# Two graph blocks on one core: the opening, the order of the steps and the last groups rearranged

## The chip, the cores and the metric

The kernel runs on one core of one Trainium2 chip. The metric is the device time of one execution in microseconds (us). Engines are named as in the profile: PE is TensorE (PEld its weight loads), DVE is VectorE, ACT is ScalarE, POOL is GpSimd, SP is SyncE, which here only issues DMAs.

## The reference, cut to what matters

There are 128 graphs of 128 nodes with 256 features, and an adjacency of zeros and ones. Two layers follow each other.

```python
# layer 0: attention with 8 heads; only edge types 0 and 1 occur in adj
q, k = src @ Wq + bq, src @ Wk + bk
attn = softmax(q k^T / sqrt(32))
out  = sum_r (attn * (adj == r)) @ (src @ Wv[r] + bv[r])
x = LN(src + out @ Wo + bo)
x = LN(x + gelu(x @ W1 + b1) @ W2 + b2)            # 256 -> 1024 -> 256
# layer 1: two graph attention steps, then a relu feed-forward
def gat(h, W, a):                                   # softmax over axis 1, the source nodes
    Wh = h @ W
    e = leaky_relu(Wh @ a[:256] + (Wh @ a[256:])^T, 0.2)
    return softmax(where(adj > 0, e, NEG), axis=1) @ Wh
h = LN(x + gat(gat(x, W1g, a1), W2g, a2))
out = LN(h + relu(h @ w_ff1 + b_ff1) @ w_ff2 + b_ff2)
```

## The kernel before

**Tiling.** All is in float32. Four graphs (512 tokens) make a group; there are 32 groups. One group's work is cut into generators, and each `yield` ends a step:

- `projections` has 8 steps: two for the queries, two for the keys (L560), four for the values (`pv`, L570, with the bias added on DVE at L574).
- `attention` has 12: for each pair of graphs `scores` (matmuls L588, four exponentials L594), `masked` (DVE, L602), and three of `sums` (denominators L615, weighted values L624, reciprocals and products on DVE); then two with the output projection L662, the residual and its statistics.
- `ffn` has 22: 14 with the products of the first matrix (`product`, L400, each four passes of 256 columns) and 8 of the second (`product2`, L409, 16 passes of 128). It is a seven-product form of a 2x2 block product, so most products add into one PSUM bank, `seeded`, and ACT copies stand between them (L438, L445 `p7`, L449 `p16`, L472). `first_ffn` uses gelu, `second_ffn` relu.
- `layer1` has 12: two with `Wh` (L713), `spread`, three of `edges`, the product L726, `spread`, three of `edges`, the product L738 with residual and statistics.
- `norm` has 4: `root` (DVE L324, POOL power L325), `normed` (L333 on DVE, then L338 on ACT, one instruction for each graph; for the last norm L343 on DVE), and two of `scaled` (DVE, L356). `turned` transposes the normalised group on PE (L290), copies it on ACT (L293) and forms sums for the next products (L378 to L381, DVE).

**Graph weights.** `graph_weights` makes one matrix `wu` from the weights of both graph steps, so that one product gives what both need. It runs once, in the opening, with columns on DVE (L92), four transposes (L254) and a product (L262) on PE. Its sources lie in `temp`, which is the later `hT` buffer.

**Spread.** `spread` lays one number per node along the free axis in all partitions: a transpose on PE (L672), a copy on DVE (L674), a DMA to HBM (L677) and a DMA back to all partitions (L678). The 64 return trips are issued on SP.

**Order.** `manual_schedule` keeps the order of the text on every engine. `in_order` takes a list of generators, with a count of steps where it is over one, and runs them; so the kernel's schedule is written out by hand. In the loop over `g`, the first list holds `first_ffn` of group g+1 (`f1`) with the graph steps of group g (`l1`); the second holds `second_ffn` of group g (`f2`) with the attention of group g+2 (`at`, `pr`). PSUM tiles with tag `s` come from a ring of four banks; each new tile waits until the one four before it has been read.

Of the kernel before, what the change touches and what calls it, by code (L numbers as in the profile page):

```python
# [23 lines left out]
P = 128  # L24
# [5 lines left out]
class Weights:  # L30
# [55 lines left out]
    def columns(self, wt, arow, scr, name):  # L86

        nch, d = wt.shape[1], wt.shape[2]
        wa = self.tile([P, nch, 2], "wa_" + name)
        for c in range(nch):  # L90
            for s in range(2):
                self.nc.vector.scalar_tensor_tensor(  # L92
                    scr, wt[:, c, :], 1.0, arow[:, s * d : (s + 1) * d],
                    op0=ALU.mult, op1=ALU.mult, accum_out=wa[:, c, s : s + 1],
                )
        return wa
# [10 lines left out]
def fast_pass(ctx, tc, a, out):  # L107
# [47 lines left out]
    def entered(g):  # L155

        xt = load_xT(g)
        ad, xr = load_rest(g)
        return dict(xt=xt, ad=ad, x=xr, g=g)
# [3 lines left out]
    first = dict(g=0, xt=load_xT(0))  # L163
# [49 lines left out]
    gw1, gw2 = (k.w("L1_gnn_W" + s, cut(NCH, D)) for s in "12")  # L213
    a1, a2 = (k.row("L1_gnn_a" + s, t=cut(2 * D)) for s in "12")
# [7 lines left out]
    w2 = forms("L0_gnn_W2")  # L222
    g2c, be2c = k.col("L0_gnn_g2"), k.col("L0_gnn_beta2")
# [13 lines left out]
    NU = D + 4  # L237
    wu = k.tile([P, NCH, NU], "wu")

    def graph_weights():  # L240

        scr = cut(D)
        wa1 = k.columns(gw1, a1, scr, "1")
        wa2 = k.columns(gw2, a2, scr, "2")
        rhs = cut(NCH, D + 2)
        nc.vector.tensor_copy(rhs[:, :, :D], gw2)
        nc.vector.tensor_copy(rhs[:, :, D : D + 1], wa2[:, :, 1:2])
        nc.vector.tensor_copy(rhs[:, :, D + 1 : D + 2], wa2[:, :, 0:1])
        gw1T = cut(NCH, D)
        yield  # L250
        for m in range(NCH):
            pt = mm_tile(f"pgt_{m}")
            for c in range(NCH):
                nc.tensor.transpose(  # L254
                    pt[:, c * P : (c + 1) * P], gw1[:, c, m * P : (m + 1) * P], k.ident
                )
            nc.scalar.copy(gw1T[:, m, :], pt[:, :D])
        yield
        for m in range(NCH):
            pu = mm_tile(f"pgw_{m}")  # L260
            for c in range(NCH):
                nc.tensor.matmul(  # L262
                    pu[:, : D + 2], gw1T[:, c, m * P : (m + 1) * P], rhs[:, c, :],
                    start=(c == 0), stop=(c == NCH - 1),
                )
            nc.scalar.copy(wu[:, m, : D + 2], pu[:, : D + 2])
            nc.vector.tensor_copy(wu[:, m, D + 2 : D + 3], wa1[:, m, 1:2])
            nc.vector.tensor_copy(wu[:, m, D + 3 :], wa1[:, m, 0:1])
        yield
# [57 lines left out]
    def normed(S, i, bs=slice(0, G)):  # L327


        x, mv, rs = S["x"], S["mv", i], S["rs", i]  # L330
        if i < 3:
            sh = small.tile([P, G], F32, tag="sh", name=f"sh_{i}_{S['g']}")
            nc.vector.scalar_tensor_tensor(  # L333
                sh, mv[:, :, 0], -1.0, rs, op0=ALU.mult, op1=ALU.mult
            )
        for b in range(bs.start, bs.stop):
            if i < 3:
                nc.scalar.activation(  # L338
                    x[:, b, :], x[:, b, :], AF.Identity, bias=sh[:, b : b + 1],
                    scale=rs[:, b : b + 1],  # L340
                )
            else:
                nc.vector.tensor_scalar(  # L343
                    x[:, b, :], x[:, b, :], mv[:, b, 0:1], rs[:, b : b + 1],
                    op0=ALU.subtract, op1=ALU.mult,
                )
# [322 lines left out]
    def spread(columns, n):  # L669

        pr = ps_s.tile([P, T], F32, tag="s", name="pr_" + n)
        nc.tensor.transpose(pr[:G, :P], columns, k.ident)  # L672
        line = small2.tile([G, P], F32, tag="line", name="line_" + n)
        nc.vector.tensor_copy(line, pr[:G, :P])  # L674
        t = w2p.tile([P, G, P], F32, tag="spread", name="spread_" + n)
        hbm = dram.tile([G, P], F32, tag="hbm", name="hbm_" + n)
        nc.sync.dma_start(hbm, line)  # L677
        nc.sync.dma_start(t, hbm.partition_broadcast(P))  # L678
        return t
# [25 lines left out]
    def layer1(S):  # L705
# [14 lines left out]
        target = spread(wh[:, :, D + 3], n + "_0")  # L720
# [10 lines left out]
        target = spread(yh[:, :, D + 1], n + "_1")  # L731
# [42 lines left out]
    with tc.manual_schedule(engines={ET.PE, ET.Activation, ET.DVE, ET.SP, ET.Pool}):  # L774

        nc.tensor.matmul(seeded, k.ident, first["xt"][:, 0, :], start=True, stop=True)
# [3 lines left out]
        gw, pr, at = graph_weights(), projections(first), attention(first)  # L780
# [4 lines left out]
            lambda: combined(w1), (pr, 4), gw, (pr, 4), (at, 2), gw, at, lambda: combined(w2), at, gw, (at, 2), (pr1, 2), at,  # L785
            at, (pr1, 2), (at, 2), at, pr1, at, pr1, (n0, 2), lambda: turned(first, 0), (n0, 2),
# [4 lines left out]
            lambda: combined(u1), (f1, 4), at1, (f1, 4), at1, pr1, (f1, 3), (at1, 3), pr1, f1, at1, f1, at1,  # L791
            f1, f1, (at1, 3), f1, f1, at1, lambda: combined(u2), f1, at1, f1, n0_, f1, n0_, (f1, 2), lambda: turned(S1, 0), n1_, (n0_, 2),
        )
        for g in range(NG - 1):
# [8 lines left out]
            ready = (lambda: prepared(S2)) if more else (lambda: None)  # L803
            if g == 0:
                in_order((f1, 2), n1_, pr, (f1, 2), lambda: turned(S, 1), (n1_, 2))
                l1 = layer1(S)
                in_order(
                    f1, l1, f1, l1, f1, l1, (f1, 2), pr, (f1, 4), pr, f1, (l1, 3), f1, pr, f1, l1, f1,
                    l1, pr, f1, pr, f1, (l1, 3), f1, pr, f1, l1, n2, (at, 2), f1, n2, f1, n1, pr,
                    lambda: turned(S, 2), (at, 3),  # L810
                )
            else:
                n3 = norm(st[g - 1], 3)
                in_order(
                    pr, lambda: turned(S1, 0), pr, f1, f2_, n3, f1, n0_, (f1, 4), n0_, (f1, 2), n3, l1, f1, f1, l1, n3,
                    (f1, 3), pr, n3, lambda: store(st[g - 1]), f1, f1, exp, l1, l1, pr, f1, l1, f1,
                    f1, l1, n2, f1, at, n2, at, f1, pr, lambda: turned(S, 2), pr, (at, 3), f1, f1, pr, n1,
                )
            if not more:
# [3 lines left out]
                f2, pr, f2, n1, (n2, 2), f2, at, (f2, 2), lambda: turned(S1, 1), (f2, 2), at, (n1, 2),  # L823
                (f2, 2), l1, at, ready, (f2, 4), l1, f2, at, f2, l1, (f2, 2), at, at, f2, at, n0, l1, f2,
                n0, l1, gelu, f2, l1, f2,
            )
            n0_, f2_ = n0, f2
        in_order((f2, 2), n1, (f2, 2), lambda: turned(S1, 1), (n2, 2))
        l1 = layer1(S1)
        in_order(  # L830
            f2, (l1, 2), f2, l1, (n1, 2), (f2, 8), (l1, 3), f2, l1, f2, l1, (f2, 4), (l1, 3), f2, l1,
        )
        n2, n3 = norm(S1, 2), norm(S, 3)
        in_order(n2, f2, n2, (f2, 2), lambda: turned(S1, 2))
        f2 = second_ffn(S1)
        in_order((f2, 14), (n2, 2), (n3, 4), lambda: store(S), (f2, 2))
        checks()
        in_order((f2, 4))
        for p in (1, 0):
            root(S1, 3, pair(p))  # L840
            normed(S1, 3, pair(p))
# [3 lines left out]
            if p == 1:  # L845
                in_order((f2, 2))
# [18 lines left out]
def general_pass(ctx, tc, a, out):  # L865
# [46 lines left out]
    def gat_weights(s):  # L912
# [5 lines left out]
        nc.vector.tensor_copy(wt[:, :, D : D + 1], wa[:, :, 1:2])  # L918
        for c in range(NCH):
            nc.vector.tensor_copy(wb[:, c, :], wa[:, c, 0:1].to_broadcast([P, P]))  # L920
# [271 lines left out]
```

## Time and profile before

| what | value |
|---|---|
| median of 3 runs | 2836.33 us (2835.97 to 2838.88) |
| the profiled execution, its own time | 2840.0 us |
| its span, first to last instruction | 2837.9 us |
| PE busy | 2776.8 us, 98% |
| DVE, ACT, POOL busy | 77%, 55%, 6% |
| mean granted clock of TensorE | 0.991 |
| moved by DMA | 87.27 MB |

The span is the time between the first and the last instruction that the profile shows; 2.1 us of the execution's own time lie around it. The profiled execution took 3.7 us more than the median. Busy time of PE counts a matmul as long as the profile's model holds it in the array, so a busy PE isn't always one at its peak. The clock is given as a share of the full one; a 0.5 means that each pass takes twice as long.

### The profile page before, as it was taken

What the parts mean: (1) busy time and instruction counts of PE and PEld (TensorE: products, weight loads), DVE (VectorE), ACT (ScalarE), POOL (GpSimd) and SP (SyncE); (2) the same over time, 40 slices, a digit from 0 to 9 for tenths busy, and PEclk for the clock granted to TensorE, in tenths of its full rate; (3) what the DMA queues carried; (4) which work ended last, traced back from release to release, by engine and by line L of the source; (5) the groups of instructions that cost most, each with busy time, mean ns of one, the idle gap of its engine ahead of it and who ended that gap; (6) DMA issues with size and microseconds to landing.
All of it is one profiled execution on the core that took longest, in us unless ns stands there. A gap on an engine that the chain in (4) does not pass through costs nothing.

```text
span 2837.9 us, 51798 instructions
## 1 busy us (share of the span) xinstructions
PE 2776.8 (98%) x20816; PEld 2233.8 (79%) x20816; DVE 2176.8 (77%) x5068; ACT 1568.5 (55%) x3395; POOL 162.2 (6%) x153
## 2 busy tenths in 40 slices
PE   8999999999999999999999999999999999999986
PEld 4778788887888887888887887887887887888875
DVE  6677887877787877777877777778778778878765
ACT  3545555556555556555556565556556555555552
POOL 3000000000000000000000000000000000000000
PEclk9999999999999999999999999999999999999998
DMA  6010110010111010111010111000110001110000
GB/s 173 5 27 15 32 35 34 24 34 12 34 35 34 23 35 12 35 34 34 23 35 12 35 34 34 24 26 21 34 35 27 31 15 32 35 34 23 16 16 20
DMA packets 70645, 87.27 MB, mean 31 GB/s; under 512 B 8192, under 2 KB 48512, under 8 KB 70400
## 3 DMA queue, kind: packets, MB, share of 16 engines
q1 hardware_dynamic: 69568, 83.52, 9.5%
q8 instruction: 164, 2.69, 0.4%
q14 instruction: 81, 0.66, 0.1%
q10 hardware_dynamic: 832, 0.40, 0.0%
HBM read 66.99 MB, written 16.91 MB: 30 GB/s over the span
## 4 chain that ended last, share of the span: by engine, by line
PE 86%; ACT 7%; DVE 2%; issue 0%; POOL 0%; POOLq 0%; DVEq 0%; ACTq 0%
PE ph L400 14%; PE po L409 14%; PE seeded L409 12%; PE seeded L400 11%; PE pq L560 7%; PE pv L570 6%; PE pw L713 4%; PE pav L624 4%; ACT x L338 4%; PE pwo L662 4%; PE pt L290 3%; PE pden L615 2%; PE py L726 2%; PE pg L738 2%; ACT e L594 1%; PE ps L588 1%
## 5 line engine op out<-in xcount | busy, mean ns | idle before, releaser
L338 ACT ACTIVATE x<-x,sh,rs 128x256 f32<-128x256 f32 x384 | 199.4, 597 | 180.5 <-DVE sh L333 180.5
L325 POOL TENSOR_TENSOR rs<-rs,mhalf 128x4 f32<-128x4 f32 x129 | 138.8, 1076 | 2635.0 <-DVE rs L324 2225.5
L594 ACT ACTIVATE e<-ps 128x512 f32<-128x512 f32 x256 | 131.8, 601 | 209.1 <-PE ps L588 209.1
L570 PE MATMUL pv<-wv,xT 128*128 128x512 f32 x512 | 242.3, 597 | 0.3 <-ACT e L594 0.3
L400 PE MATMUL seeded<-yS,w_L_gnn_w_ff 128*128 128x256 f32 x768 | 207.3, 392 | 5.0 <-ACT seeded L472 1.3
L400 PE MATMUL seeded<-yS,w_L_gnn_W 128*128 128x256 f32 x768 | 204.0, 388 | 2.4 <-ACT seeded L472 1.3
L455 DVE TENSOR_TENSOR hT<-seeded,p 128x512 f32<-128x512 f32 x128 | 88.5, 692 | 148.3 <-PE seeded L400 148.3
L400 PE MATMUL ph<-yT,w_L_gnn_w_ff 128*128 128x256 f32 x768 | 199.0, 388 | 0.0
L310 DVE BATCH_NORM_STATS2 st<-x 128x6 f32<-128x256 f32 x512 | 192.5, 418 | 7.7
L400 PE MATMUL ph<-yT,w_L_gnn_W 128*128 128x256 f32 x768 | 194.4, 382 | 2.4 <-ACT yT L293 2.4
L409 PE MATMUL po<-w_L_gnn_W,hT 128*128 128x128 f32 x1536 | 190.1, 277 | 0.0
L409 PE MATMUL po<-w_L_gnn_w_ff,hT 128*128 128x128 f32 x1536 | 187.0, 275 | 0.0
L409 PEld LDWEIGHTS po<-w_L_gnn_w_ff,hT 128*128 128x128 f32 x1536 | 184.0, 192 | 3.2
L409 PEld LDWEIGHTS po<-w_L_gnn_W,hT 128*128 128x128 f32 x1536 | 181.7, 192 | 5.7 <-issue 0.5
L400 PEld LDWEIGHTS seeded<-yS,w_L_gnn_W 128*128 128x128 f32 x768 | 138.4, 190 | 52.7 <-issue 15.6
L400 PEld LDWEIGHTS seeded<-yS,w_L_gnn_w_ff 128*128 128x128 f32 x768 | 137.8, 190 | 48.9 <-ACT p L449 24.6
L400 PEld LDWEIGHTS ph<-yT,w_L_gnn_W 128*128 128x128 f32 x768 | 144.2, 191 | 38.0 <-ACT yT L293 10.2
L400 PEld LDWEIGHTS ph<-yT,w_L_gnn_w_ff 128*128 128x128 f32 x768 | 139.2, 191 | 38.3 <-issue 13.9
L602 DVE TENSOR_TENSOR pm<-e,adj 128x512 f32<-128x512 f32 x256 | 161.7, 693 | 4.1 <-ACT e L594 4.1
L686 ACT ACTIVATE gs<-spread,wh 128x128 f32<-128x128 f32 x128 | 40.9, 390 | 187.1 <-DMA spread<-hbm 187.1
L424 ACT ACTIVATE hT<-hT,c_L_gnn_b 128x256 f32<-128x256 f32 x256 | 109.4, 497 | 61.4 <-DVE hT L455 60.3
L570 PEld LDWEIGHTS pv<-wv,xT 128*128 128x128 f32 x512 | 90.7, 192 | 66.1 <-issue 63.6
(155 smaller groups left out, 6116.4 us busy)
## 6 DMA issues: line engine op xcount, KB each, us to landing
xT<-in_xT_dram SPq DMA_DIRECT2D x32, 512.0 KB, 7.1
x<-in_x_dram SPq DMA_DIRECT2D x32, 512.0 KB, 8.3
spread<-hbm SPq DMA_DIRECT2D x64, 256.0 KB, 4.2
out_dram<-x SPq DMA_DIRECT2D x31, 512.0 KB, 2.9
adj<-in_adjT_dram SPq DMA_DIRECT2D x32, 256.0 KB, 6.0
w_L_gnn_W<-in_L_gnn_W_dram SPq DMA_DIRECT2D x8, 256.0 KB, 7.3
w_L_gnn_w_ff<-in_L_gnn_w_ff_dram SPq DMA_DIRECT2D x8, 256.0 KB, 5.1
hbm<-line SPq DMA_DIRECT2D x64, 2.0 KB
```

The costliest lines, as they stand in the source:

```text
L310: nc.vector.bn_stats(st[:, b % 2, :], S["x"][:, b, :])
L325: nc.gpsimd.tensor_tensor(rs[:, bs], rs[:, bs], k.mhalf[:, bs], op=ALU.pow)
L338: nc.scalar.activation(x[:, b, :], x[:, b, :], AF.Identity, bias=sh[:, b : b + 1], scale=rs[:, b : b + 1],)
L400: nc.tensor.matmul(bank[:, s * TH : (s + 1) * TH], wa[:, form, 0, f * P : (f + 1) * P], m, start=start and s == 0, stop=True, skip_group_c ...
L409: nc.tensor.matmul(bank[:, s * P : (s + 1) * P], m[:, f, s * P : (s + 1) * P], wb_[:, form, f, :], start=start and s + f == 0, stop=True, ...
L560: nc.tensor.matmul(pq, w[:, c, m * P : (m + 1) * P], xt[:, c, :], start=(c == 0), stop=(c == NCH - 1),)
L570: nc.tensor.matmul(pv, xt[:, c, b * P : (b + 1) * P], wv[:, c].rearrange("p r d -> p (r d)"), start=(c == 0), stop=(c == NCH - 1),)
L594: nc.scalar.activation(e[:, s], pss[s], AF.Exp, scale=SCALE)
L602: nc.vector.tensor_mul(pm[:, s], S["e", p][:, s], S["ad"][:, pair(p), None, :].to_broadcast([P, 2, NCH, P]),)
L624: nc.tensor.matmul(pav[s * DH : (s + 1) * DH, u, c, :], v[:, d0 : d0 + DH], m[:, s, u, c, :], start=(r == 0), stop=(r == 1),)
L662: nc.tensor.matmul(po[:, s * D : (s + 1) * D], oT[:, c, b * P : (b + 1) * P], wo[:, c, :], start=(c == 0), stop=(c == NCH - 1),)
L713: nc.tensor.matmul(pw[:, :NU], yT[:, c, b * P : (b + 1) * P], wu[:, c, :], start=(c == 0), stop=(c == NCH - 1),)
```

## The change

- **Opening.** Instead of one product that waits for the first input, four products of the identity with itself fill `seeded`. The first pair's scores come directly behind the keys, ahead of the values. The graph weights leave the opening: their four loads go behind the second group's inputs and the weights `w2`, into the buffers of `wh` and `yh`, and their steps (now four: columns 1, columns 2, transposes, products) stand in the first group's feed-forward. The two extra columns of the product are now matmuls of their own. The second group's first scores, mask and sums move ahead of the first feed-forward; a gelu table is loaded ahead of it.
- **Spread.** With `direct`, `spread` is four matmuls with the broadcast column as weights and the identity as moving operand, whose result is read from PSUM. This is used for both spreads of groups 0 and 31 and for the second one of group 30.
- **Loop.** In the first list, the second of two value steps moves ahead of `turned(S, 2)`. In the second list a value step moves behind the second step of `f2` and `normed` of `n1`.
- **Last groups.** The transposes of group 30's last norm go behind `f1`'s last steps; a step of `f2` moves from before to behind the transposes of group 31; the lists from there on are written anew; the last norm is applied on ACT where only a pair is normed.

The core of the diff:

```diff
@@ entered
-        return dict(xt=xt, ad=ad, x=xr, g=g)
+        return dict(xt=xt, ad=ad, x=xr, g=g, direct={NG - 1: 0, NG - 2: 1}.get(g, 2))
@@ loads
-    gw1, gw2 = (k.w("L1_gnn_W" + s, cut(NCH, D)) for s in "12")
-    a1, a2 = (k.row("L1_gnn_a" + s, t=cut(2 * D)) for s in "12")
     wo = k.w("L0_gnn_Wo")
...
     second = entered(1)
     w2 = forms("L0_gnn_W2")
+    gw = flat(w1p.tile([P, G, NU], F32, tag="wh", name="gw"))[...]
+    ga = flat(w1p.tile([P, G, D + 2], F32, tag="yh", name="ga"))[...]
+    for i in range(2):
+        k.w(f"L1_gnn_W{i + 1}", gw[:, i])
+        k.row(f"L1_gnn_a{i + 1}", t=ga[:, i])
@@ graph_weights, last step
+            for cols, rhs in ((slice(0, D), gw[:, 1]), (slice(D, D + 2), wa2)):
+                for c in range(NCH):
+                    nc.tensor.matmul(pu[:, cols], gw1T[:, c, m * P : (m + 1) * P], rhs[:, c, :], ...)
@@ normed
-        if i < 3:
+        scalar = i < 3 or bs.stop - bs.start < G
+        if scalar:
@@ spread
+        if direct:
+            for b in range(G):
+                nc.tensor.matmul(
+                    pr[:, b * P : (b + 1) * P], columns[:, b : b + 1].to_broadcast([P, P]), k.ident,
+                    start=True, stop=True,
+                )
+            return pr.rearrange("p (b i) -> p b i", b=G)
@@ the schedule
-        nc.tensor.matmul(seeded, k.ident, first["xt"][:, 0, :], start=True, stop=True)
+        for _ in range(4):
+            nc.tensor.matmul(seeded, k.ident, over(k.ident), start=True, stop=True)
-            lambda: combined(w1), (pr, 4), gw, (pr, 4), (at, 2), gw, at, lambda: combined(w2), at, gw, (at, 2), (pr1, 2), at,
-            at, (pr1, 2), (at, 2), at, pr1, at, pr1, (n0, 2), lambda: turned(first, 0), (n0, 2),
+            lambda: combined(w1), (pr, 4), at, (pr, 2), at, (pr, 2), at, lambda: combined(w2), (at, 3), (pr1, 2),
+            (at, 2), (pr1, 2), (at, 3), pr1, at, at1, n0, n0, pr1, at1, lambda: turned(first, 0), (at1, 2),
@@ first feed-forward
-            lambda: combined(u1), (f1, 4), at1, (f1, 4), at1, pr1, (f1, 3), (at1, 3), pr1, f1, at1, f1, at1,
-            f1, f1, (at1, 3), f1, f1, at1, lambda: combined(u2), f1, at1, f1, n0_, f1, n0_, (f1, 2), lambda: turned(S1, 0), n1_, (n0_, 2),
+            gelu, lambda: combined(u1), (f1, 4), pr1, f1, f1, at1, at1, f1, pr1, f1, n0, at1, (f1, 2), n0, f1, at1,
+            (f1, 3), gwu, at1, f1, gwu, f1, at1, gwu,
+            f1, at1, f1, gwu, at1, lambda: combined(u2), f1, n0_, f1, n0_, (f1, 3), lambda: turned(S1, 0), n1_, (n0_, 2),
@@ the loop, first list from group 1 on (its last line)
-                    f1, l1, n2, f1, at, n2, at, f1, pr, lambda: turned(S, 2), pr, (at, 3), f1, f1, pr, n1,
+                    f1, l1, n2, f1, at, n2, at, f1, pr, pr, *((ahead,) if more else ()), (at, 3), f1,
+                    f1, pr, n1, *(() if more else (ahead,)),
@@ the loop, second list (its first line)
-                f2, pr, f2, n1, (n2, 2), f2, at, (f2, 2), lambda: turned(S1, 1), (f2, 2), at, (n1, 2),
+                (f2, 2), n1, pr, (n2, 2), f2, at, (f2, 2), lambda: turned(S1, 1), (f2, 2), at, (n1, 2),
@@ the last groups
-        in_order((f2, 2), n1, (f2, 2), lambda: turned(S1, 1), (n2, 2))
+        in_order(f2, n1, (f2, 2), lambda: turned(S1, 1))
-            f2, (l1, 2), f2, l1, (n1, 2), (f2, 8), (l1, 3), f2, l1, f2, l1, (f2, 4), (l1, 3), f2, l1,
+            (f2, 2), (l1, 3), f2, l1, (f2, 2), l1, n1, (f2, 2), l1, n1, (f2, 2), l1, f2, l1, n2, f2, l1, l1, n2, (f2, 3), l1, (f2, 2), l1,
-        in_order(n2, f2, n2, (f2, 2), lambda: turned(S1, 2))
+        in_order(n2, f2, n2, (f2, 3), lambda: turned(S1, 2))
-        in_order((f2, 14), (n2, 2), (n3, 4), lambda: store(S), (f2, 2))
+        in_order(f2, n3, (f2, 3), n2, n3, (f2, 4), n2, n3, (f2, 4), n3, lambda: store(S), (f2, 2))
```

In the first loop pass (g = 0) the lists are rewritten in the same way: the graph steps start after six steps of `f1` instead of four, and its end is that of the later passes. The very last norm is split: both roots come early, and pair 0 is normed while pair 1 is scaled and stored.

## The prediction

> **What bounds the kernel now.** I read the page first, then busy time by stretch, PE's waits in each stretch, and the timeline where a wait stands. By the page PE bounds the kernel at nearly full clock:
>
> ```profile
> PE 2776.8 (98%) x20816; PEld 2233.8 (79%) x20816; DVE 2176.8 (77%) x5068; ACT 1568.5 (55%) x3395; POOL 162.2 (6%) x153
> ```
>
> The stretches (bounds, length, busy time and count of PE, PEld, DVE, ACT and POOL, then clock and DMA) show where the other 2% are: PE lacks 20.0 us in the first 180, 3.9 in 2485 us of the middle, 37.3 in the last 173.
>
> ```profile
> 0.00:180.00 180.00, 159.98 (x1137) 110.81 (x1138) 114.08 (x240) 84.75 (x168) 28.79 (x29) 0.96 0.26 72
> 180.00:2665.00 2485.00, 2481.10 (x18846) 2006.67 (x18845) 1954.83 (x4552) 1413.73 (x3074) 125.62 (x116) 1.00 0.09 29
> 2665.00:2838.00 173.00, 135.67 (x836) 116.31 (x834) 107.86 (x278) 70.01 (x156) 7.75 (x8) 0.89 0.05 16
> ```
>
> A wait costs twice, for the clock follows it. Two throttled stretches, one of each end:
>
> ```profile
> 55.00:62.00 7.00, 6.80 (x17) 4.59 (x18) 4.63 (x4) 3.62 (x6) 6.69 (x6) 0.52 0.00 0
> 2785.80:2792.80 7.00, 6.37 (x17) 4.38 (x18) 1.61 (x4) 4.11 (x7) 0.00 (x0) 0.51 0.00 0
> ```
>
> Each follows a wait of about 4 us. PE's waits of the opening, then those of the end (who, for whom: us, times, longest):
>
> ```profile
> PE pt L290 <- ACT x L338: 6.0, 12, 3.8
> PE seeded L776 <- DMA xT<-in_xT_dram: 5.2, 1, 5.2
> ...
> PE pt L290 <- ACT x L338: 6.4, 8, 4.0
> PE seeded L409 <- DVE x L496: 4.8, 1, 4.8
> PE pg L738 <- DVE gs L702: 4.4, 2, 3.1
> PE py L726 <- DVE gs L702: 4.3, 1, 4.3
> ```
>
> In the middle the page shows no wait, for each is under 0.15 us by its model. The timeline shows two per period of 85.73 us. The eight transposes take 1.30 us where those at 1033.67 take 1.04; the products at 1032.70 start 1.22 us after those before them, where four passes take 0.86:
>
> ```profile
> 1016.68 1.30 PE L290 MATMUL pt<-ident,x 128*128 128x128 f32 x8
> 1031.48 1.13 PE L400 MATMUL ph<-yT,w_L_gnn_w_ff 128*128 128x256 f32 x4
> 1032.08 0.57 ACT L449 COPY p<-seeded 128x512 f32<-128x512 f32 x1
> 1032.70 1.13 PE L400 MATMUL seeded<-yS,w_L_gnn_w_ff 128*128 128x256 f32 x4
> ```
>
> The copy L449 comes late since the four normalisations L338 hold ACT from 1030.10 to 1032.18.
>
> **What the Trainium skill says.** "TensorE: Matmul & The Clock Gate", Part 1 (the HAM clock gate): the clock starts at half and rises after some 3.4 us of sustained work in a free-running window, and falls after an idle one. The trace agrees: passes of 512 columns start 0.85 us apart until about 10.9 us, 0.43 after. "ScalarE: Activation LUTs", What ACT_TABLE_LOAD costs, gives 1.28 us; here it is 1.28. "SBUF — State Buffer", section on its two sides: DVE with two SBUF inputs and GpSimd exclude each other. The four masks L602 agree: 4.83 us beside POOL's `combined`, 2.49 otherwise.
>
> **The change part by part.**
>
> *Opening, to 62 us.* (1) Identity products: the identity is ready at 1.3 us (POOL), so PE starts at 1.4 rather than 5.15. Eight passes: seven at 0.85, if the clock rises at about 7.5 (one window earlier than now), one at 0.43, end 7.8. Queries and keys then take 16 x 0.43 = 6.9 and end at 14.7; now 15.8. Gain 1.1. Bounds: rise at 4.8 gives 2; no rise before 8.2 and the products delay the queries by 1.2. (2) Scores behind the keys wait for the last key copy (0.69 us on ACT, 0.4 beyond the first scores), and the values behind them for a bank until the first exponential is out (0.85). Now the same places wait 0.36 + 0.48: loss 0.4. (3) The graph weights' 2.9 us of PE only move. The two-column products add eight short passes, 0.11 each by the 128-column passes: 0.9. Their eight column instructions on DVE (8 x 0.47) go beside a feed-forward where DVE has a third free. Their four SP loads (256 KB each, 1 MB) are moved past `wo`, `w1`, group 1's inputs and `w2`, which land earlier; the weights aren't needed until some 85 us. (4) Ahead of the first norm's transposes stand now 1.7 us of scores and 1.7 of values, so of 3.85 + 0.32 us about 1.1 stays. But the masks stand ahead of L378-381 on DVE, and POOL's `combined` runs then (10.9 us): the sums wait some 2.7 us for them. The throttled 6.8 us should go: 3.4. Net 4.2 − 3.8 + 3.4 = 3.8. Sum: 1.1 − 0.4 − 0.9 + 3.8 = 3.6.
>
> *First feed-forward and first pass, 62 to 180.* Now its exponentials come amid gelus: three table loads between 63.4 and 70.2 us, and PE waits 0.86 + 1.26. With those scores gone and gelu loaded ahead, both go: 2.1. In the pass: the product L726 waits 0.86 for the spread's trip, which goes; at 155 to 166 us waits of 2.5 and 6.8 us at half clock (3.1 of work lost) go by the loop's order; 1.1 at L449 (174.3) too. Two direct spreads cost 2 x (8 x 0.11 − 0.11) = 1.6. Its first edge exponential now falls amid gelus, two loads of 1.28; the copies behind it have 6.9 us of products as cover, so I cost it at nothing. If the cover fails, 1 to 2 us. Sum 2.1 + 0.86 + 2.5 + 3.1 + 1.1 − 1.6 = 8.1. With 1.5 off for waits that I don't see, the opening gives 3.6 + 8.1 − 1.5 = **10** (bounds 3 and 15).
>
> *Middle.* A value step (1.72 us) ahead of the transposes: normalised rows are all there by 1017.2, PE arrives at 1018.4, and 0.21 to 0.26 go. The denominators behind them wait for no one new: ACT reaches L632 at about 1020.85, now 1020.76. In the second list L333 no longer stands behind a value's addition on DVE, so the normalisations start at 1028.8 instead of 1030.1, L449 runs at 1030.9, and the products at 1032.3 find it done: 0.25. What waits newly: that value's addition (L574) frees the fourth score bank at 1030.3, just when the scores come. Scale steps behind it have a us of slack. So 0.46 x 29 passes = **13** (bounds 8 and 17).
>
> *End, from 2665.* Waits by the list sum to 23.3 without the final flag. Group 31's chain is what counts. The order holds its first edges behind `f2`'s step 14, so L702 ends at 2760.45 and PE stood 4.25 us; the DMA trip (2747.1 to landing, about 5 us) is hidden there anyway. New: transposes of group 30's norm go behind 1.8 us of `f1` (now a wait of 1.37), so group 31's norm starts about 3.5 us earlier; edges follow at once after a direct spread. I count what stays: 1.3 at L738 of group 30, 1.3 at L472, 1.8 at the moved transposes, 1.5 where masks and DVE's feed-forward sums meet, 1.0 elsewhere: 7. Gone: 16. The wait of 4.8 for `x` L496 goes since the two norms' scale steps on DVE are spread over 14 products instead of standing ahead of it. Seven throttled stretches (27 us at half) lose 12 now; I let half stay: 6. Three direct spreads: −2.3. The last norm's two pairs overlap: from PE's last `po` to the last scale 9.75 us now, by the same durations 8.2 (ACT's 2 x 0.52 for DVE's 0.73 included): 1.3. Sum 16 + 6 − 2.3 + 1.3 = 21, less 1 for DVE: **20** (bounds 8 and 27).
>
> Total 10 + 13 + 20 = 43. Against the profiled execution, 2840.0: 2797. The median of the runs is 3.7 lower, 2836.3: 2793; as late waits tend to come back, I say **2794**.
>
> **The rivals.**
> - *Chains, not PE.* Group 31's graph steps are DVE and ACT work at both ends, and POOL's lock stretches the masks. For: DVE at 67.42 of 85.70 us in a period. Against: the direct spreads. Opening 4, middle 13, end 9: 2810.
> - *The middle doesn't move.* The small gaps are the pipeline's own and reappear at the next copy. Against: the like products at 1037.21 run without. 10 + 20: 2806.
> - *A new wait per pass, slower.* The score ring: were the moved value's addition to come out of DVE behind the two scale steps (2.6 us), scores would wait in 29 passes. It decides from 30/29, about 1.0 us a pass; at 2 us it gives −30 + 58: 2864. Against: in program order the addition stands ahead of the scale steps, and L333 ahead of it waits only for POOL's 1.01.
> - *The first products don't warm the clock*: that part turns to a loss of 1.2, within the first case.
>
> **How the numbers follow.** First case 0.72, chains 0.15, middle still 0.08, new wait 0.03, and 0.02 that losses cancel. A measurement of this kernel can tell about 0.2% from no change (5.7 us). So faster 0.95, same 0.02, slower 0.03. The first case alone is 2780 to 2804; the range reaches over the two weaker gains: 2778 to 2815.
>
> **What would show it.** Queries ending near 14.7 us; no half clock at 55 to 62 and 157 to 164 us; a period of 85.3 instead of 85.73 and transposes of 1.04 us throughout; no spread trips in groups 0 and 31; PE's waits behind 2665 near 7 us, and fewer throttled stretches. A period of 85.7 or more, or a wait of PE at L588 for L574 in each pass, would prove me wrong in the middle; waits of over 12 us at the end, there.

## The result, and the profile after

The changed kernel takes **2787.17 us** (median of 4 runs, 2786.80 to 2787.80); beside it on the same chip the kernel before took 2837.61 (2835.97 to 2839.44). The ratio is **0.9822, 95% interval 0.9805 to 0.9839**. The profiled execution took 2787.48 us, its span is 2785.6. Line numbers are higher by 7 to 23 now: L400 is L408, L338 is L346, L449 is L457, L472 is L480, L602 is L610, L702 is L718, L726 is L742, L738 is L754.

The page's PE, then the three stretches, whose bounds stand where the same steps start as before (columns as before: bounds, length, busy time and count of PE, PEld, DVE, ACT, POOL, clock, DMA share, GB/s):

```profile
PE 2751.0 (99%) x20865; PEld 2238.1 (80%) x20865; DVE 2181.2 (78%) x5055; ACT 1574.4 (57%) x3401; POOL 164.3 (6%) x153
```
```profile
0.00:171.80 171.80, 157.69 (x1165) 111.16 (x1166) 116.31 (x232) 84.26 (x170) 30.44 (x29) 0.99 0.26 72
171.80:2637.20 2465.40, 2465.40 (x18850) 2015.80 (x18849) 1960.01 (x4553) 1420.19 (x3075) 125.61 (x116) 1.00 0.09 29
2637.20:2785.60 148.40, 127.94 (x854) 111.10 (x852) 104.90 (x272) 69.90 (x158) 8.25 (x8) 0.97 0.04 14
```

In the middle PE now has no idle time at all; before it lacked 3.9 us. PE's busy time falls by 25.8 us although the trace counts 49 matmuls more, so about half of what was won is not idle time but the same products taking less time. The end's clock is 0.97 where it was 0.89.

To divide the gain I use the starts of the second graph product `pg` of groups 1 and 29 in the two timelines:

| stretch | before | after | won | predicted |
|---|---|---|---|---|
| start to `pg` of group 1 | 236.79 | 228.63 | 8.2 | 10 |
| 28 periods to `pg` of group 29 | 28 x 85.73 | 28 x 85.03 | 19.7 | 13 |
| from there to the end | 200.69 | 176.20 | 24.5 | 20 |
| sum | 2837.93 | 2785.61 | 52.3 | 43 |

The medians differ by 50.4 us, 1.9 less than the spans of the two profiled executions. One profile is one execution: that of the kernel before took 3.7 us more than the median of its first three runs and 2.4 more than that of the four here, that of the kernel after 0.3. So some 2 to 3 us of the 52.3 are not the change's; the section on the end shows where they lie. PE's longest waits of the first 180 us (who, for whom: us, times, longest):

```profile
PE pav L632 <- DVE pm L610: 3.7, 5, 1.3
PE pv L578 <- ACT e L602: 2.4, 3, 1.5
PE pt L297 <- ACT x L346: 2.3, 10, 0.6
```

The transposes' 6.0 us of before are down to 2.3, and PE first waits 1.4 us for the identity instead of 5.2 for the first input; the masks L610 are new at the head.

### The profile page after: what moved, and what is told of

It reads as the page before. It is cut to its first block, busy times and chain, and to the rows that moved or that the text cites. A ratio compares the mean times of both kernels' runs of the same rounds, so it can differ in the third digit from the quotient of the medians.

```text
span 2785.6 us, 51902 instructions
## 1 busy us (share of the span) xinstructions
PE 2751.0 (99%) x20865; PEld 2238.1 (80%) x20865; DVE 2181.2 (78%) x5055; ACT 1574.4 (57%) x3401; POOL 164.3 (6%) x153
## 4 chain that ended last, share of the span: by engine, by line
PE 94%; DVE 2%; ACT 1%; DMA 1%; SPq 1%; issue 0%; POOL 0%; ACTq 0%; DVEq 0%; POOLq 0%
PE po L417 16%; PE ph L408 16%; PE seeded L408 12%; PE seeded L417 12%; PE pv L578 7%; PE pq L568 7%; PE pw L729 4%; PE pav L632 4%; PE pwo L670 4%; PE pt L297 3%; PE ps L596 2%; PE pden L623 2%; PE py L742 2%; PE pg L754 2%; ACT x L346 0%; DVE x L364 0%
## 5 line engine op out<-in xcount | busy, mean ns | idle before, releaser
L346 ACT ACTIVATE x<-x,sh,rs 128x256 f32<-128x256 f32 x388 | 201.6, 596 | 200.0 <-DVE sh L341 200.0
L602 ACT ACTIVATE e<-ps 128x512 f32<-128x512 f32 x256 | 131.5, 597 | 207.9 <-PE ps L596 207.9
L578 PE MATMUL pv<-wv,xT 128*128 128x512 f32 x512 | 235.7, 593 | 2.4 <-ACT e L602 2.4
L408 PE MATMUL seeded<-yS,w_L_gnn_w_ff 128*128 128x256 f32 x768 | 204.2, 388 | 3.0 <-ACT seeded L480 2.2
L408 PE MATMUL seeded<-yS,w_L_gnn_W 128*128 128x256 f32 x768 | 203.5, 387 | 1.9 <-ACT seeded L446 0.9
L408 PE MATMUL ph<-yT,w_L_gnn_w_ff 128*128 128x256 f32 x768 | 196.3, 385 | 0.5 <-ACT yT L300 0.4
L408 PE MATMUL ph<-yT,w_L_gnn_W 128*128 128x256 f32 x768 | 192.7, 380 | 0.6 <-ACT yT L300 0.4
L408 PEld LDWEIGHTS seeded<-yS,w_L_gnn_w_ff 128*128 128x128 f32 x768 | 140.1, 190 | 48.7 <-issue 14.1
L408 PEld LDWEIGHTS seeded<-yS,w_L_gnn_W 128*128 128x128 f32 x768 | 138.0, 189 | 51.0 <-issue 15.5
L408 PEld LDWEIGHTS ph<-yT,w_L_gnn_W 128*128 128x128 f32 x768 | 143.2, 190 | 36.1 <-ACT yT L300 7.9
L408 PEld LDWEIGHTS ph<-yT,w_L_gnn_w_ff 128*128 128x128 f32 x768 | 141.2, 191 | 34.4 <-issue 14.3
L610 DVE TENSOR_TENSOR pm<-e,adj 128x512 f32<-128x512 f32 x256 | 166.9, 713 | 0.0
L702 ACT ACTIVATE gs<-spread,wh 128x128 f32<-128x128 f32 x120 | 38.3, 390 | 189.4 <-DMA spread<-hbm 189.4
```

The lines of the kernel that those rows point to most:

```text
L346: nc.scalar.activation(x[:, b, :], x[:, b, :], AF.Identity, bias=sh[:, b : b + 1], scale=rs[:, b : b + 1],)
L408: nc.tensor.matmul(bank[:, s * TH : (s + 1) * TH], wa[:, form, 0, f * P : (f + 1) * P], m, start=start and s == 0, stop=True, skip_group_c ...
L578: nc.tensor.matmul(pv, xt[:, c, b * P : (b + 1) * P], wv[:, c].rearrange("p r d -> p (r d)"), start=(c == 0), stop=(c == NCH - 1),)
L602: nc.scalar.activation(e[:, s], pss[s], AF.Exp, scale=SCALE)
L610: nc.vector.tensor_mul(pm[:, s], S["e", p][:, s], S["ad"][:, pair(p), None, :].to_broadcast([P, 2, NCH, P]),)
```

## The experiments

Times in each group of runs are set against the kernel before on the same chip (medians 2836.3 to 2838.6). Differences from the kernel after are small, so they are read in the traces first, at the steps of the table above.

### The middle: each edit by itself

The kernel before with one list edit, then with both:

```diff
-  f1, l1, n2, f1, at, n2, at, f1, pr, lambda: turned(S, 2), pr, (at, 3), ...
+  f1, l1, n2, f1, at, n2, at, f1, pr, pr, lambda: turned(S, 2), (at, 3), ...    # e1 and e2
-  f2, pr, f2, n1, (n2, 2), f2, at, ...
+  (f2, 2), n1, pr, (n2, 2), f2, at, ...                                         # e2 alone
```

> The kernel before with one edit: in the first list of the later passes the second value step stands ahead of turned(S, 2). Theory: only the wait of the eight transposes L290 goes (1.30 us back to 1.04): the period from 85.73 to 85.47, about -7.5 us in 29 passes, and the products that start 1.22 us late behind the copy p16 stay. Rival (the small gaps are the pipeline's own and come back elsewhere): transposes shorter, period unchanged at 85.7, time unchanged.

> The kernel before with both edits of the middle (the value step ahead of turned(S, 2); in the second list a value step behind the second step of f2 and n1). Nothing else of the change. Theory from the kernel after: the whole difference of the period is these two edits, so 85.03 instead of 85.73, about -20 us (29 x 0.70). Rival (the prediction's sum): 85.27, -13 us, and the other 0.24 a pass comes from elsewhere in the change.

**Measured:** e1 2829.59 us, ratio 0.9974 (0.9965 to 0.9983), period **85.47**; e2 2815.27 us, ratio 0.9926 (0.9913 to 0.9940), period **85.03**, the period of the kernel after. So the first edit is worth 0.26 a period and the second 0.44, and nothing else of the change is seen in the middle. The timeline of e1 around the products of the second edit (start, length, engine, line, operation, count):

```profile
1029.00 1.13 PE L400 MATMUL ph<-yT,w_L_gnn_w_ff 128*128 128x256 f32 x4
1030.22 1.13 PE L400 MATMUL seeded<-yS,w_L_gnn_w_ff 128*128 128x256 f32 x4
1031.19 1.04 PE L290 MATMUL pt<-ident,x 128*128 128x128 f32 x8
1032.06 1.97 PE L400 MATMUL ph<-yT,w_L_gnn_w_ff 128*128 128x256 f32 x8
1033.87 1.03 PE L400 MATMUL seeded<-yS,w_L_gnn_w_ff 128*128 128x256 f32 x4
```

The transposes have their 1.04 us, the wait at 1030.22 still stands. The same steps in the kernel after:

```profile
1016.74 1.13 PE L408 MATMUL ph<-yT,w_L_gnn_w_ff 128*128 128x256 f32 x4
1017.71 1.03 PE L408 MATMUL seeded<-yS,w_L_gnn_w_ff 128*128 128x256 f32 x4
1018.57 1.04 PE L297 MATMUL pt<-ident,x 128*128 128x128 f32 x8
1019.44 1.89 PE L408 MATMUL ph<-yT,w_L_gnn_w_ff 128*128 128x256 f32 x8
1021.17 1.03 PE L408 MATMUL seeded<-yS,w_L_gnn_w_ff 128*128 128x256 f32 x4
```

From start to start: 1.22 becomes 0.97 (0.25, the wait that I had counted). But the four products behind it also fall from 0.97 to 0.86, and the eight after the transposes from 1.81 to 1.73. That is 0.25 + 0.11 + 0.08 = 0.44. PE's weight loads in e1 show where the other 0.19 comes from:

```profile
1030.22 0.73 PEld L400 LDWEIGHTS seeded<-yS,w_L_gnn_w_ff 128*128 128x128 f32 x4 [0.49 <-ACT p L449]
1032.90 0.73 PEld L400 LDWEIGHTS ph<-yT,w_L_gnn_w_ff 128*128 128x128 f32 x4 [0.21 <-ACT hT L424]
```

The first load waits for the copy too and starts together with its product at 1030.22, so that the second product starts 0.32 us after the first; the others follow at 0.22, with their loads one product ahead. That is the 0.11. The second load waits 0.21 us for another instruction of ACT, which runs half a microsecond later against PE here than in the kernel after: this costs the 0.08. In the kernel after the copy is done before PE arrives at 1017.71, and neither wait is there:

```profile
1016.51 0.56 ACT L457 COPY p<-seeded 128x512 f32<-128x512 f32 x1
```

A wait of a quarter of a microsecond came with nearly as much again behind itself. The theories with 85.47 and 85.03 hold, the sum of the prediction (85.27) and the rival that gaps come back don't.

### The end: order and direct spreads apart

e3 takes the direct spreads away and keeps every order; e5 keeps them and puts the last groups' lists (and the last norm) back:

```diff
-  return dict(..., direct={NG - 1: 0, NG - 2: 1}.get(g, 2))      first = dict(g=0, direct=0, ...
+  return dict(..., direct=2)                                     first = dict(g=0, direct=2, ...     # e3
-  (f2, 2), (l1, 3), f2, l1, (f2, 2), l1, n1, (f2, 2), l1, n1, ...
+  f2, (l1, 2), f2, l1, (n1, 2), (f2, 8), (l1, 3), f2, l1, ...                                        # e5, and the lists around it
```

> The kernel after with all four spreads of groups 0 and 31 and the second of group 30 through HBM again; all orders kept. Theory: the end's order now runs group 31's edges straight behind its Wh, so each round trip of about 5 us through HBM is only partly covered: +6 to +12 us at the end, 0 to +2 in the opening. Rival (trips are hidden by the order, as they were before the change): PE is spared the direct products, 1.6 us in the opening and 2.3 us at the end, so -2 to -4 us.

> The kernel after with the lists of the last groups (and the last norm's engine) as in the kernel before; opening, middle and all direct spreads stay. Theory (order first: a direct spread is worth something only where edges may start behind it): in the old order the trips were hidden, so direct spreads alone only cost their 2.3 us of products, the end's whole gain of 24.5 us goes and the time rises by 22 to 27 us. Rival (the two add: e3_no_direct lost 8.8 us at the end, so direct spreads are worth that in any order): +15 to +16 us.

**Measured:** e3 2798.90 us, ratio 0.9865 (0.9850 to 0.9880); e5 2811.10 us, ratio 0.9908 (0.9893 to 0.9923). The time from `pg` of group 29 to the end, with e2 as the kernel that has both edits of the middle and nothing else:

| | trips through HBM | direct |
|---|---|---|
| old order | 196.4 (e2) | 198.2 (e5) |
| new order | 185.0 (e3) | 176.2 (after) |

e5 is 23.9 us above the kernel after, as its theory had it; that the two parts add (+15) is refuted. Direct spreads in the old order **cost 1.8 us**; in the new order they **win 8.8**. The order alone wins 11.4, both 20.2. PE's waits of e5 in that stretch (who, for whom: us, times, longest) are those of before, the product L742's among them:

```profile
PE pt L297 <- ACT x L346: 7.1, 8, 4.7
PE seeded L417 <- DVE x L504: 4.8, 1, 4.8
PE py L742 <- DVE gs L718: 4.3, 1, 4.3
PE pg L754 <- DVE gs L718: 4.2, 2, 3.1
```

In the old order the trip is not what the edges wait for. Their first instruction on ACT follows straight on a feed-forward instruction, with no wait for the landing (kernel before):

```profile
2754.92 0.81 ACT L424 ACTIVATE hT<-seeded,c_L_gnn_b_ff 128x256 f32<-128x256 f32 x2
2755.63 1.27 ACT L686 ACTIVATE gs<-spread,wh 128x128 f32<-128x128 f32 x4
```

So to shorten the trip won nothing there. In e3 the edges do wait for it, and there it appears under another name. Waits of PE, then ACT's timeline in e3:

```profile
PE seeded L408 <- ACT seeded L480: 4.6, 2, 3.9
...
PE seeded L417 <- ACT seeded L495: 3.4, 1, 3.4
```
```profile
2718.62 0.91 ACT L432 ACTIVATE hT<-hT,c_L_gnn_b_ff 128x256 f32<-128x256 f32 x2 [1.96 <-DVE hT L467]
2721.69 1.28 ACT L702 ACTIVATE gs<-spread,wh 128x128 f32<-128x128 f32 x4 [2.17 <-DMA spread<-hbm]
2722.88 0.81 ACT L432 ACTIVATE hT<-seeded,c_L_gnn_b_ff 128x256 f32<-128x256 f32 x2
2723.72 0.57 ACT L480 COPY seeded<-ph 128x512 f32<-128x512 f32 x1
```

The list says that PE waits for a copy of the feed-forward. The copy is late because the edge instruction L702 stands ahead of it on ACT and waits 2.17 us for the landing. As ACT runs its instructions in the order of the schedule, the name in the wait list is the last link, not the cause. Of the 8.8 us, 5.9 are PE's waits (15.0 instead of 9.1 without the flag's) and 3.0 its busy time, at a mean clock of 0.93 instead of 0.97. The end's 8.8 us are as its theory expected; in the opening it expected 0 to 2, and `pg` of group 1 is 3.7 us later than in the kernel after, with a wait of 3.1 us for L480 there too.

These positions come from one execution each. The medians tell the same: from e2 to e5, less the 7.1 us that `pg` of group 1 comes earlier, the direct spreads cost 2.9; e3 is 11.7 above the kernel after, which leaves 8.0 for the end.

e2 also shows how much of the end's 24.5 us is the change's. It keeps the old order and the old spreads, and yet its end is 4.3 us shorter than that of before (196.4 against 200.7). PE's waits are the same there (24.0 against 23.3 us without the flag's), but its busy time is 5.1 us less: the clock record has half clock for 17 us ahead of PE's last products, where that of before has 27. The medians, 21.2 us apart, leave no room for these 4.3: the periods give 19.7 (28 x 0.70) and the opening 1.1, so about 0.4 stays for the end. By the medians, then, most of the 4.3 is that one execution of the kernel before, which lay 3.7 us above its median, and not the change; no second profile of it shows this directly. Against e2, whose profiled execution lies within 0.4 us of its median, the end wins **20.2**.

### The opening: its parts undone one at a time

```diff
-  for _ in range(4):
-      nc.tensor.matmul(seeded, k.ident, over(k.ident), start=True, stop=True)
+  nc.tensor.matmul(seeded, k.ident, first["xt"][:, 0, :], start=True, stop=True)     # e4
-  (pr, 4), at, (pr, 2), at, (pr, 2), at, lambda: combined(w2), ...
+  (pr, 8), (at, 3), lambda: combined(w2), ...                                        # e6
+  (pr, 4), (gwu, 2), at, (pr, 2), at, (pr, 2), gwu, at, ..., at, gwu, (at, 2), ...   # e7; its loads ahead of wo
```

> The kernel after with the opening product of before (one, waiting for the first input) in place of four identity products. Theory: the clock rises near 11 us again, the keys end near 15.8 instead of 13.5, and all behind is 2.3 us later; at the second group's product pg 230.9 instead of 228.6. Rival (the opening's later waits take it up): under 0.5 us left at pg.

> The kernel after with all four value steps ahead of the first pair's scores, as in the kernel before; else the same. Theory (exponentials and masks of the first pair start 3.5 us earlier when scores stand first, and the first sums wait for them): first sums wait again, +0.5 to +3 us at the second group's product pg. Rival (the prediction's sum: scores directly behind the keys only add waits of 0.4 us): -0.4 us, nothing that the time shows.

> The kernel after with the graph weights' loads ahead of wo, as in the kernel before, and their four steps among the first group's sums; all else stays. Theory (1 MB ahead of wo, w1 and the second group's inputs, and DVE's eight columns and PE's 2.9 us beside the first masks): the second group's first product is later by 1 to 3 us and the first masks and sums wait for DVE: +1 to +4 us at pg of the second group. Rival (the products only move, and in the opening they fill waits of PE): -1 to -3 us, for they would then stand in idle time.

| kernel | median us | ratio, 95% interval | first `pq` | `pg` of group 1 |
|---|---|---|---|---|
| after | 2787.17 | 0.9822 (0.9805 to 0.9839) | 6.65 | 228.63 |
| e4, one product | 2788.20 | 0.9828 (0.9815 to 0.9842) | 7.10 | 230.04 |
| e6, values first | 2787.53 | 0.9826 (0.9812 to 0.9839) | 6.51 | 227.90 |
| e7, weights early | 2790.40 | 0.9835 (0.9822 to 0.9848) | 7.32 | 231.56 |

None of these times alone can be told from the kernel after; the positions in the traces can, within limits. The first `pq` follows the identity products without a gap, so in the kernel after, e6 and e7 its start shows only when the clock rose: the passes go from 0.85 to 0.43 us at 4.9, 4.6 and 6.3 us. This differs before anything else does, and I take it off. Past that, three executions with the same opening (the kernel after, e3 and e5) start the second group's feed-forward at 105.52, 104.94 and 105.48 us, so less than 0.6 us can't be told. **e4:** the first key product is 2.2 us later, `pg` 1.4: the identity products win about 1.4 us up to there, between my two theories: later waits take up the rest of what the keys lost. PE's first lines in the kernel after:

```profile
1.37 5.45 PE L794 MATMUL seeded<-ident 128*128 128x512 f32 x8 [1.37 <-POOL ident masks.py:199]
6.65 3.60 PE L568 MATMUL pq<-xT,w_L_gnn_Wq 128*128 128x512 f32 x8
```

Eight passes in 5.28 us: at 0.85 and 0.43 us a pass that is four to five slow ones, so the clock rose near 5 us and all of the queries run at full speed. **e6:** with values first `pg` is 0.6 us earlier, once the start is taken off, no more than what executions of the same opening differ by. The scores directly behind the keys win nothing that can be seen here: my theory of earlier exponentials fell. **e7:** 2.9 later, 2.3 without the start. PE stands 3 us at the first sums:

```profile
PE pden L623 <- DVE v L582: 3.0, 1, 3.0
```

My theory had the first masks and sums wait for DVE's columns. But the eight columns are done at 17.9 us, and DVE then waits 0.84 us for PE's first values. What holds the value additions up are the masks ahead of them on DVE, and these are slow beside POOL's `combined`. In the kernel after, then in e7:

```profile
15.90 5.31 POOL L211 TENSOR_TENSOR w_L_gnn_W<-w_L_gnn_W 128x512 f32<-128x512 f32 x4 [14.59 <-DMA w_L_gnn_W<-in_L_gnn_W_dram]
20.44 3.66 DVE L610 TENSOR_TENSOR pm<-e,adj 128x512 f32<-128x512 f32 x4
```
```profile
18.98 5.96 POOL L211 TENSOR_TENSOR w_L_gnn_W<-w_L_gnn_W 128x512 f32<-128x512 f32 x4 [17.67 <-DMA w_L_gnn_W<-in_L_gnn_W_dram]
21.10 5.52 DVE L610 TENSOR_TENSOR pm<-e,adj 128x512 f32<-128x512 f32 x4
```

With the graph weights' loads ahead, the first feed-forward's weights land 3 us later, POOL starts 3 us later, and more of its work lies beside the masks. Loads and steps moved together are worth about 2.3 us; the trace points to the loads, but no run moves them alone.

### What still held the opening back

The prediction let the half clock at 55 to 62 us go. In the profile of the kernel after, half of it is still there. That kernel at 52 to 60 us, then its masks (count, ns at least, median, most):

```profile
52.00:60.00 8.00, 5.80 (x77) 3.88 (x76) 8.00 (x6) 4.19 (x8) 7.69 (x6) 0.79 0.01 2
```
```profile
L610 DVE TENSOR_TENSOR pm<-e,adj x4: 1129/1749/1760, 50.1 to 54.5; 128x512 f32<-128x512 f32 x4
```

POOL runs `combined` of `u1` and `u2` from 48.09 for 12.14 us without a break. DVE's masks need 6.16 us in place of 2.49, PE waits 0.94 and 1.26 us for them, and 56 to 60 us run at 0.57 of the clock. The clock is the smaller part of what is lost here, though. e4 shows half clock behind the same two waits too, but e3, e5 and e6, which also have them, run at 1.00 from 56 to 60 us. They then wait 0.69 us ahead of the products of `seeded` (60.74 us in e3), which in the kernel after come without a wait at 61.31. e3, level with the kernel after up to 56 us, is 0.6 us ahead there. So the half clock costs some 0.6 us, and not in every execution. What all of them share is that DVE is late beside POOL. e8 moves both combinations into the first pass of the loop, e9 makes them on DVE:

```diff
-  gelu, lambda: combined(u1), (f1, 4), ...    gwu, at1, lambda: combined(u2), f1, ...
+  gelu, (f1, 4), ...                          gwu, at1, f1, ...                                    # e8 and e9
+  ... lambda: turned(S, 1), lambda: combined(u1), lambda: combined(u2), f1, (n1_, 2), f1           # e8
+  (f1, 3), lambda: summed(u1), gwu, ...       (f1, 2), lambda: summed(u2), exp, ...                # e9: nc.vector.tensor_sub
```

> The kernel after with POOL's two combinations u1 and u2 out of the first feed-forward and behind turned(S, 1) of the first loop pass. Theory (POOL's 12 us excludes DVE from its masks: 6.16 us for four in place of 2.49, and PE waits 0.94 + 1.26 us for them and runs at half clock behind): masks back to 2.5 us, those two waits and the half clock at 56 to 60 us gone, -3 to -4 us at the second group's product. Rival (the masks are late anyway, since DVE is behind with sums and transposes' copies): masks shorter, but under 1 us gained.

> The kernel after with the combinations of u1 and u2 on DVE instead of POOL, four instructions ahead of the first step of the graph weights, four ahead of exp in the first loop pass. Since e8_masks_free won 4 us up to the second feed-forward and lost them when POOL's 12 us then lay beside DVE's scale steps. Theory (POOL's lock on DVE was the cost in both places): 8 DVE instructions of about 0.68 us, 5.5 us in stretches where DVE has a third or more free, and no lock: -3 to -5 us at the second group's pg and in the time. Rival (DVE has no room there either, or a later wait takes up what is won): within 1 us of the kernel after.

**Measured:** e8 2788.91 us, ratio 0.9828 (0.9815 to 0.9842); e9 2784.77 us, ratio 0.9819 (0.9805 to 0.9832). In e8 the first product of the second group's feed-forward starts at 101.21 instead of 105.52, so the 4 us are there, although the clock rose 0.6 us later. Then POOL stands beside the scale steps L364, one of which takes up to 1.75 us instead of 0.68; DVE's chain is late, and PE's longest wait of e8 between 45 and 160 us, with the stretches around it, is

```profile
PE pr L683 <- ACT wh L733: 2.9, 1, 2.9
```
```profile
116.00:120.00 4.00, 1.09 (x6) 0.68 (x5) 2.99 (x5) 1.83 (x6) 0.39 (x1) 0.84 0.00 0
120.00:124.00 4.00, 4.00 (x14) 3.46 (x14) 1.83 (x3) 1.32 (x5) 0.00 (x0) 0.50 0.00 0
124.00:128.00 4.00, 4.00 (x13) 2.46 (x12) 0.00 (x0) 2.35 (x5) 0.00 (x0) 0.80 0.00 0
```

(Bounds, length, the five engines, clock, DMA share, GB/s.) The spread's products wait 2.9 us, 2.2 more than in the kernel after, and the half clock around them, to 125.6 us, costs 2.8 more. Another stretch of half clock, from 101.7 to 105.1 us, took 1.7; it begins ahead of POOL's part (104.6). `pg` of group 1 comes at 231.56, later than in the kernel after (2.3 without the start). Both theories for e8 missed: the masks were the cost, and the cost moved with POOL. The Trainium skill ("SBUF — State Buffer", SBUF: two separate sides) has a DVE instruction with two SBUF inputs and a GpSimd one that reads SBUF exclude each other for a whole instruction; masks and scale steps both read two tiles from SBUF, and both show it here (up to 1.76 and 1.75 us instead of 0.68). e9, without POOL's part, keeps the gain: masks in 2.49 us again, neither of the two waits for them, and `pg` at 225.54, **3.1 us earlier**, at the lower end of what its theory gave. Against e3 at the start of the second group's feed-forward (102.40 for 104.94), where e3 had no half clock either, it is 2.5.

```profile
50.68 2.49 DVE L614 TENSOR_TENSOR pm<-e,adj 128x512 f32<-128x512 f32 x4
```

e10 adds four orders to e9, among them values first and

```diff
-  l1, l1, l1, f1, l1, f1, pr, l1,            (f2, 3), l1, (f2, 2), l1,    in_order(n2, f2, n2, ...
+  l1, l1, f1, l1, f1, l1, pr, l1,            (f2, 3), l1, f2, l1,         in_order(n2, (f2, 2), n2, ...
```

> e9_on_dve and four orders: all values ahead of the first scores (e6_values_first: -0.6); the second group's second value step ahead of its sums in the first feed-forward (PE's wait of 1.47 us behind the exponentials); a feed-forward step between Wh and the first spread of group 0 (wait of 0.68); at the end a step of f2 moved between the two scale steps of group 31's norm (wait of 1.81 us ahead of its transposes, and some half clock behind it). Theory: these waits have no other work ready only because of the order, so -3 to -5 us beyond e9_on_dve, 2778 to 2782. Rival (the chain of DVE and ACT behind each sets the time, a PE step in the gap only moves the wait): within 1 us of e9_on_dve.

**Measured:** 2784.89 us, ratio 0.9814 (0.9801 to 0.9828), the rival's value in the time. PE's wait for the transposes at the end falls from 1.82 to 0.41 us, but 0.79 comes at L758 in its place, and in the first feed-forward 1.47 + 0.67 become 0.36 + 1.92. The span of its profile is 1.7 us below that of e9 (2781.2 against 2782.9), but this execution lies 1.9 us under its own median, so nothing beyond e9 is shown. e9 and e10 lie 2.4 and 2.3 us below the kernel after in the median. The times can't tell 0.1%; that e9 is better is shown by the position of `pg`.

## Why the prediction was right, and where its sizes were off

The case forecast as likeliest, PE's waits with the clock behind them, came true, at 2787.2 instead of 2794: 52.3 us of span in place of 43, or some 49 to 50 by the medians.

**Opening: 10 predicted, 8.2 measured.** The waits were well counted: ahead of the first norm's transposes 0.59 + 3 x 0.16 = 1.1 us stay (1.1), the sums wait 0.94 + 1.26 = 2.2 for the masks (2.7). The keys end at 13.5 us and not at 14.7, since the clock rose near 5 us and not at 7.5; of the 2.2 us that the identity products win at the keys, 1.4 reach `pg` (e4), where 1.1 was predicted. Three terms failed:
- "1.5 off for waits that I don't see": the gaps that came are 1.47 at a value product (70.36 us), 0.67 at L408 (74.73) and 0.69 at the first spread (119.33), 2.8 together. The first two fill the place of the 2.1 us of waits that were to go from the first feed-forward.
- "1.1 at L449 (174.3) too": of this wait 0.82 stays (167.25).
- "The throttled 6.8 us should go: 3.4." Half of it came back in the profiled execution and cost about 0.6; in e3, e5 and e6 it was gone. What didn't go is DVE's lateness beside POOL, which e9 prices at 2.5 to 3.1; the prediction took this wait for the masks as given.

Together they bring the 10 to about 8. The direct spreads, 1.6 of PE against 0.86 of trip, were set against the old order. In the new one the opening would be 3.7 us later without them (e3): they are a condition of the order here as at the end, which the prediction doesn't say for the opening.

**Middle: 13 predicted, 19.7 measured.** Both edits do what was said, and no new wait came: L596, the scores behind the moved value, is not in the list, and the stretch has no idle time. The first edit is worth 0.26 (predicted 0.21 to 0.26). The term that was too small is the second: 0.25 was the start of the late products alone. The weight load that starts with its product (0.11) and the second wait behind the same late ACT (0.08) were in the timeline of before, as 1.13 and 1.97 us of products against 1.03 and 1.89, and I had not compared them.

**End: 20 predicted, 24.5 between the two profiles, 20.2 against e2.** PE's waits of the kernel after from `pg` of group 29 on:

```profile
PE pflag L881 <- DVE good L879: 4.1, 1, 4.1
PE pt L297 <- ACT x L346: 3.8, 10, 1.8
PE seeded L408 <- ACT seeded L480: 2.2, 2, 1.5
PE pg L754 <- DVE gs L718: 1.2, 1, 1.2
PE seeded L408 <- ACT seeded L446: 0.9, 1, 0.9
PE py L742 <- DVE gs L718: 0.4, 1, 0.4
PE ph L408 <- ACT yT L300: 0.4, 1, 0.4
PE pt L297 <- DVE st L317: 0.2, 1, 0.2
```

Without the flag 9.1 us stay where I had said 7; 14.2 of 23.3 are gone (16). From the end of PE's last `po` to the last scale it is 8.3 us now and was 9.6, the 1.3 predicted (its own 9.75 and 8.2 would have made it 1.55); a further 1.8 is won behind the last scale, where the span ends 4.4 instead of 6.2 us later, for which the prediction has no term and the runs no cause. PE's busy time was to fall by 6 − 2.3 = 3.7. Against the profile of before it falls by 7.6 (163.3 to 155.7), but 5.1 of these stand between before and e2, whose order at the end is the same; against e2 it falls by 2.6. One throttled stretch is left ahead of the last products:

```profile
2742.00:2749.00 7.00, 4.62 (x16) 3.07 (x15) 4.53 (x18) 3.72 (x7) 1.04 (x2) 0.77 0.00 0
```

So the sum of the end was right within a microsecond, with a little too much for waits and clock and nothing for what follows the last scale.

The sentence that the trip "is hidden there anyway" was right for the old order (e5: direct spreads cost 1.8 there, predicted 2.3), and so was that edges "follow at once after a direct spread" in the new one, which e3 prices at 8.8.

**The rivals.** Chains alone (2810) gave too little at the end; chains do hold the 9.1 us that stay. That the middle doesn't move (2806) is refuted by e1 and e2. The new wait per pass (2864) did not come. The identity products do warm the clock: it rises at 4.9 us, and at 10.5 in e4.

## What to carry to other kernels

Price a short wait by the start-to-start times of what follows too: a wait of 0.25 us came with 0.19 more, from a weight load that it held up and from a second wait for the same late engine. A long wait can bring half clock behind it: in e8 a wait 2.2 us longer brought 2.8 more. But look at other runs of the same code before a throttled stretch is priced: the one at 56 us followed the same waits in two profiles and not in three others, and cost little.

A shorter path for a transfer and an order that uses it belong together: alone the one lost 1.8 us and the other won 11.4, together 20.2. When work is moved to an idle engine, ask whose memory access it blocks; moved once more it blocks the next, and only on another engine (e9) was it gone. Loads that delay such work move the blocking too (e7).

Before a gain is divided by the traces, compare each profiled execution with the median of its kernel: here some 4 us of the end's 24.5 lay in one long execution of the kernel before and not in the change.

## What the runs showed that I had not expected

- Four products of 256 columns start 0.97 us apart behind a wait of 0.25 us, 0.86 without one; the difference stands in the first of them, whose weight load starts with it instead of ahead of it.
- Beside POOL's uninterrupted subtractions a mask of 128 x 512 takes up to 1.76 us on DVE, 0.68 alone; before I had seen 4.83 us for four, here 6.16.
- A wait of 1.47 us (68.89 to 70.36 us) left the clock at 1.00. Single waits of 2.9 us (e8), 3.0 (e7) and 3.1 (e3) brought 0.50 around them or behind. 0.94 + 1.26 close together brought 0.57 in the kernel after, half clock in e4 too, and nothing in e3, e5 and e6. The Trainium skill ("TensorE: Matmul & The Clock Gate", Part 1) names an idle window of some 3.4 us for the fall; these waits are shorter, and the measurement decides.
- From 1 to 5 us the clock column shows 1.00, while passes of 512 columns take 0.85 us there. At the very start the passes tell the clock, not the column.
